# Gates of 32 early steps for the last 128 features of all batches, one stage earlier, in a recurrent kernel on one Trainium2 core

## The chip, the cores and the metric

The kernel runs on one core of a Trainium2 chip. Its engines are named as in the profile: PE (TensorE, matmuls; PEld is its weight load), DVE (VectorE), ACT (ScalarE), POOL (GpSimd) and SP (SyncE, which here issues nearly all DMAs). The metric is the device time of one execution in microseconds (us); lower is better. Everything is float32.

## The reference

Input x has 16 batches, 512 steps and 512 features; a condition vector of 512 features goes with each batch. Four layers, each added to its input:

```python
x = x + (x + x * sigmoid(silu(cond @ W1.T + b1) @ W2.T + b2))     # what the first layer comes to here
x = x + hs          # h_t = tanh(x_t @ Wx + h_{t-1} @ Wh + b), h_0 = cond
x = x + hidden      # gated scan, below
x = x + x + x @ (base + A_b @ B_b.T)     # A_b, B_b: rank 8, made from cond by a small network
```

The third layer is the one that the change touches:

```python
forget_gate = sigmoid(x @ W_f.T + b_f)
input_gate  = sigmoid(x @ W_i.T + b_i)
gate_sum = forget_gate + input_gate + EPS
forget_norm = forget_gate / gate_sum
new_info = input_gate / gate_sum * (x @ W_h.T + b_h)
# hidden: a scan over the 512 steps with forget_norm + EPS and new_info, started from cond
```

`forget_norm` and `new_info` at a step depend only on x of that step, so they can be made as soon as the second layer has that step. The scan itself needs all steps.

## The kernel before

Features lie on partitions in KC = 4 chunks of 128; x2 (the input of the third layer) stays in SBUF as [128, 4, 16 batches, 512 steps].

**The recurrence.** 512 steps in NBLK = 64 blocks of T = 8 steps. One step on PE is 16 recurrent products (`accumulate`, line 371, with `wh_sb`; in the profile L371 pre<-wh_sb,h_out; 32 matmul records), then ACT takes tanh in four pieces (L535), DVE transposes them into h (L536), and only then can the next step's recurrent matmuls start. Engines work through their instructions in program order, which is written out by hand here. Between the recurrent matmuls of two steps PE is given other work, the filler of a step, in this order:
- `inputs` of the next block: 16 units a block, divided among the steps by SHARE (lines 480 to 487);
- `layer_part` (line 318; matmuls L332): in blocks 0 to 16, four times a block, one layer of the network that makes A and B. Its weights come in chunks of 256 KB, loaded AHEAD = 3 chunks ahead by `load_chunk` (L316), each load issued when a chunk has been used;
- `early_gate` (line 402; matmuls L418): one quarter (one of four 128-feature products) of a gate for the early steps.

**Early gates.** SETS lists which (batches, steps, feature chunk j) are made during the recurrence. A set is always 512 columns (batches times steps) and takes 12 calls of `early_gate`: four for the forget gate, four for the input gate, four for the candidate. PARTS says at which steps of a block a call stands: none in the first FIRST = 8 blocks, then steps 0, 2, 4 up to block 16, and steps 0, 2, 4, 6 afterwards. A set's sums, reciprocals and products are cut into 16 pieces, which `do_pieces` puts on DVE one a step, behind the step's transposes. The results go to `early` in DRAM (L435) and are loaded again later. The first two sets take 8 batches of 64 steps; they use one PSUM buffer only ("pg"), since the other ("pf") still serves `layer_part`. The tiles `ef`, `ei` and `es` have one buffer each.

**Ends of blocks.** After step 7 of a block n: `end_layer(n)` (line 342) copies a layer's result into a tile "got" (one buffer, DVE, L347) and stores it (four DMAs, L349); two 128-row chunks of the third layer's weights are loaded (L564), wf in blocks 2 and 3, wi in 4 and 5, wc in 6 and 7, base in 8 and 9; and after block 2 `turn_bias` (line 358) transposes the bias b2a on PE, copies it on DVE into another "got" (L363) and stores it (L365). All these DMAs are issued by SP, in this order.

**The batches.** After the recurrence, for each of 16 batches four `gate_unit`s (line 585), one for each feature chunk j: 12 products on PE over the columns from `te` on (L591; `te` is what `made_before` says was made early), two sigmoids, a chain on DVE (among it the reciprocal L608 and three scans over 512 steps), two additions on POOL. `make_layer` (L645, L648) and `last_layer` (L655, 13.7 us of matmuls a batch) of the batch before lie between the units.

Of the kernel before, what the change touches and what calls it, by code (L numbers as in the profile page):

```python
# [30 lines left out]
F32 = mybir.dt.float32  # L31
# [4 lines left out]
P = 128  # L36
B, S, D = 16, 512, 512
KC = D // P
R = 8

T = 8
# [11 lines left out]


WIDE = 512
FIRST, MAIN = 64 // T, 128 // T + 1
SETS = [(slice(8, 16), slice(0, 64), j) for j in (0, 1)]
SETS += [(slice(b, b + 4), slice(0, 128), j) for b in (0, 4) for j in range(KC)]
SETS += [(slice(b, b + 4), slice(0, 128), j) for b in (8, 12) for j in (2, 3)]
SETS += [(slice(b, b + 4), slice(64, 192), j) for b in (8, 12) for j in (0, 1)]  # L60

PARTS = [()] * FIRST + [(0, 2, 4)] * (MAIN - FIRST) + [(0, 2, 4, 6)] * (NBLK - MAIN - 1) + [(0, 2, 3, 4, 6)]
# [15 lines left out]
def kernel(  # L78
# [54 lines left out]
    w2pool = rnn.enter_context(tc.tile_pool(name="w2pool", bufs=1))  # L133
# [72 lines left out]
    with tc.tile_pool(name="pre", bufs=1, side="right") as pre, tc.tile_pool(  # L206
        name="ps_pre", bufs=1, space=PSUM
# [92 lines left out]
    ps_q = rnn.enter_context(tc.tile_pool(name="ps_q", bufs=1, space=PSUM))  # L300
# [57 lines left out]
    def turn_bias():  # L358

        turned = ps_q.tile([P, P], F32, tag="pg", name="b2a_turned")  # L360
        nc.tensor.transpose(turned, b2a_raw.rearrange("p k r -> p (k r)"), ident)
        got = w2pool.tile([P, P], F32, tag="got", name="b2a_got")
        nc.vector.tensor_copy(got, turned)  # L363
        for c in range(KC):
            nc.sync.dma_start(out=bias_a[:, c * P : (c + 1) * P], in_=got[c * BP : c * BP + R, :])  # L365
# [33 lines left out]
    def early_gate(q, step):  # L399

        u, k = divmod(q, KC)
        number, which = divmod(u, 3)
        batches, steps, j = SETS[number]
        shape = dict(b=batches.stop - batches.start, t=steps.stop - steps.start)
        first = number < 2
        if k == 0:

            pool, tag = ((ps_q, "pg"), (ps_p, "pf"))[0 if first else u % 2]
            early_gate.ps = pool.tile([P, WIDE], F32, tag=tag, name=f"pg_{u}")
            if which == 0:  # L410
                early_gate.tiles = [
                    w2pool.tile([P, WIDE], F32, tag=name, name=f"{name}_{number}")
                    for name in ("ef", "ei", "es")
                ]
        ps = early_gate.ps
        w = (wf_sb, wi_sb, wc_sb)[which]
        for c in range(KC):
            nc.tensor.matmul(  # L418
                ps[c * BP : (c + 1) * BP, :].rearrange("p (b t) -> p b t", **shape),
                w[:, k, j * P + c * BP : j * P + (c + 1) * BP],  # L420
                x2[:, k, batches, steps],
                start=(k == 0),
                stop=(k == KC - 1),
                skip_group_check=True,
            )
        if k < KC - 1:
            return
        f, i, s = early_gate.tiles
        halves = [slice(n * WIDE // 2, (n + 1) * WIDE // 2) for n in range(2)]

        def sigmoid(gate, bias):
            nc.scalar.activation(gate, ps, AF.Sigmoid, bias=col(bias, j))

        def store(which, got):
            nc.sync.dma_start(  # L435
                out=early[batches, which, j, :, steps].rearrange("b p t -> p b t"),
                in_=got.rearrange("p (b t) -> p b t", **shape),
            )

        def total(at):  # L440
            nc.vector.scalar_tensor_tensor(s[:, at], f[:, at], EPS, i[:, at], ALU.add, ALU.add)

        def invert(at):
            nc.vector.reciprocal(s[:, at], s[:, at])

        def normalize(which, at):
            got = (f, i)[which]
            nc.vector.tensor_tensor(got[:, at], got[:, at], s[:, at], ALU.mult)
            if at is halves[1]:
                store(which, got)  # L450

        def times_candidate(at):
            nc.vector.scalar_tensor_tensor(
                i[:, at], ps[:, at], col(C_BH, j), i[:, at], ALU.add, ALU.mult
            )
            if at is halves[1]:
                pieces.extend(lambda at=at: normalize(1, at) for at in halves)

        def end_input_gate():
            sigmoid(i, C_BI)  # L460
            early_gate.sums = [lambda at=at: total(at) for at in halves]
            pieces.extend(early_gate.sums)
            for n in range(8):
                at = slice(n * WIDE // 8, (n + 1) * WIDE // 8)
                pieces.append(lambda at=at: invert(at))
            pieces.extend(lambda at=at: normalize(0, at) for at in halves)

        if which == 0:

            timed.setdefault(step if first else step + 6, []).append(lambda: sigmoid(f, C_BF))  # L470
        elif which == 1:
            timed.setdefault(step, []).append(end_input_gate)
        else:

            assert not any(job in pieces for job in early_gate.sums)
            urgent.extend(lambda at=at: times_candidate(at) for at in halves)
# [23 lines left out]
    for n in range(NBLK):  # L500
        ahead = []
        if n + 2 < NBLK:
            xs.append(new_x1(n + 2))
        for s in range(T):
            odd = s % 2
            g = next(i for i, pair in enumerate(PAIRS) if s in pair)
            for k in range(KC):
                for j in range(KC):
                    accumulate(pre, g, j, h_prev[:, k, :], wh_sb[:, k, :])
            if n == 0 and s < G - 1:  # L510
                for k in range(KC):
                    inputs(0, (s + 1) * KC + k, pre)

            if n + 1 < NBLK:
                if n == 1 and s in LATE:
                    for i in range(*LATE[s]):
                        inputs(n, i, pre)
                for i in range(*SHARE[n][s]):
                    inputs(n + 1, i, nxt)
            if s in LAYER_STEPS[n]:  # L520
                layer_part(n, LAYER_STEPS[n].index(s))
            if s in PARTS[n]:
                early_gate(made, n * T + s)
                made += 1
            a = apool.tile([P, P], F32, tag="a", name=f"a_{n}_{s}")

            h = h_out[s]
            if odd:
                turned, h_prev = h[:, :, :BP], h[:, :, B:]
            else:  # L530
                turned, h_prev = h[:, :, B:], h[:, :, :BP]
            bank, place = PLACE[g]
            for c in range(KC):
                at = slice(c * BP, (c + 1) * BP)
                nc.scalar.activation(a[:, at], pre[bank][:, place, at], AF.Tanh)  # L535
                nc.vector.transpose(turned[:, c, :], a[:, at])  # L536
            if s == max(PAIRS[g]):
                t0, t1 = PAIRS[g]
                step = t1 - t0
                at = slice(n * T + t0, n * T + t1 + step // abs(step), step)  # L540
                nc.vector.tensor_tensor(  # L541
                    x2[:, :, :, at].rearrange("p k b t -> p k t b"),
                    xs[n][:, :, t0 // 2, :, :],
                    turned.rearrange("p k (t b) -> p k t b", t=2),
                    ALU.add,
                )
            elif n + 2 < NBLK:
                gated(nc.vector, xs[n + 2], xb, s)
                if s == G - 1 and n + 3 < NBLK:
                    xb = load_x(n + 3)  # L550
            if s in BEGINS:
                if s < T - 1 and 0 < n < NBLK - 1:
                    nxt.append(begin(n + 1, BEGINS[s]))
                elif s == T - 1 and n + 2 < NBLK:
                    ahead.append(begin(n + 2, BEGINS[s]))
            do_pieces(n * T + s)
        if n < len(LAYERS):
            end_layer(n)

        for i in (2 * n - 4, 2 * n - 3):  # L560
            if 0 <= i < 4 * KC:
                which, k = divmod(i, KC)
                w_sb, w = ((wf_sb, wfT), (wi_sb, wiT), (wc_sb, wcT), (base_sb, base))[which]
                nc.sync.dma_start(out=w_sb[:, k, :], in_=w[k * P : (k + 1) * P, :])  # L564
        if n == 2 * KC + 4:
            for k in range(KC):
                diag = base_sb[:, k, k * P : (k + 1) * P]
                nc.vector.scalar_tensor_tensor(diag, ident, 2.0, diag, ALU.mult, ALU.add)
        if n == 2:
            turn_bias()  # L570
        pre, nxt = nxt, ahead
# [165 lines left out]
```

## Time and profile before

| what | value |
|---|---|
| median of 3 runs | 1641.43 us (1639.55 to 1641.94) |
| the profiled execution | 1640.39 us, its span 1638.6 us |
| recurrence: first recurrent matmul to last | 16.6 to about 914 us |
| a step without an early gate, blocks 4 to 7 | 1.64 us |
| a step with early gates in its block, blocks 17 on | 1.73 and 1.75 us in turn |
| reciprocal L608 over 384 and 320 columns | 2552 and 2153 ns |

A step's time is the distance between the first transposes (L536) of two steps in the timeline. In the profile's group rows, the text before the bar names line, engine, operation, what is written and what is read, and how often; after it stand the busy time in us and the mean of one in ns, then the idle time before these instructions and what ended it. A timeline row gives start and length in us, engine, line, operation, and in brackets the idle time before it with its releaser. A row of the table of stretches gives the stretch, its length, then the busy time and count of PE, PEld, DVE, ACT and POOL, the granted PE clock, the DMA engines' share and GB/s.

### The profile page before, as it was taken

The page shows a single profiled execution, that of the slowest core. Times are in us where ns is not written, and L with a number is a line of the kernel's source. Part 1 is how long each engine was busy: PE and PEld are TensorE (multiplying, and loading weights), DVE is VectorE, ACT ScalarE, POOL GpSimd, SP SyncE. Part 2 cuts the span into 40 slices and gives each one's busy share as a digit, 9 for nine tenths or more (in the row PEclk, how much of TensorE's full clock was granted, in tenths as well). Part 3 has the DMA queues.
Part 4 walks back from the last instruction along what each step waited for, and adds up shares of the span by engine and source line. Part 5 has one row for each costly group of instructions (what it writes and reads, how often), then busy time and mean ns, then how long its engine had stood idle before and what let it go on. Part 6 is the DMA issues. An engine that isn't in the chain of part 4 may idle for free.

```text
span 1638.6 us, 67294 instructions
## 1 busy us (share of the span) xinstructions
PE 1610.1 (98%) x29117; PEld 1135.8 (69%) x29117; DVE 1132.8 (69%) x3592; ACT 419.3 (26%) x2476; POOL 173.0 (11%) x144
## 2 busy tenths in 40 slices
PE   7899999999999999999999999999999999999998
PEld 6788888888888888888888555555555555555553
DVE  3444655565555656566565798888888888899886
ACT  3233333333333333333333111111111111111111
POOL 0000000000000000000000022212121222222221
PEclk9999999999999999999999999999999999999999
DMA  5344432111111111111110001101111111111111
GB/s 188 112 148 144 127 108 53 36 37 36 36 33 34 36 36 36 37 36 36 36 37 23 26 23 39 41 32 41 38 41 38 44 43 43 39 34 37 44 36 57
DMA packets 106042, 86.05 MB, mean 53 GB/s; under 512 B 15072, under 2 KB 84224, under 8 KB 105744
## 3 DMA queue, kind: packets, MB, share of 16 engines
q1 hardware_dynamic: 104640, 81.66, 16.3%
q8 instruction: 228, 3.74, 0.9%
q14 instruction: 70, 0.57, 0.1%
q10 hardware_dynamic: 1104, 0.08, 0.0%
HBM read 54.95 MB, written 26.76 MB: 50 GB/s over the span
## 4 chain that ended last, share of the span: by engine, by line
PE 90%; DVE 6%; issue 2%; ACT 1%; DMA 1%; POOL 0%; SPq 0%; DVEq 0%; ACTq 0%; POOLq 0%
PE pre L371 41%; PE po L655 11%; PE pg L418 11%; PE pf L591 8%; PE pi L591 8%; PE pc L591 8%; DVE s L608 1%; PE pl L645 1%; PE pf L332 1%; DVE s L620 1%; DVE s L616 1%; DVE i L619 0%; DVE h_out L536 0%; ACT a L535 0%; DVE f L622 0%
## 5 line engine op out<-in xcount | busy, mean ns | idle before, releaser
L371 PEld LDWEIGHTS pre<-wh_sb,h_out 128*32 128x32 f32 x16384 | 456.4, 110 | 157.8 <-DVE h_out L536 154.7
L371 PE MATMUL pre<-wh_sb,h_out 128*32 128x128 f32 x16384 | 548.1, 274 | 10.4 <-DVE h_out L536 6.3
L536 DVE STREAM_TRANSPOSE h_out<-a 128x32 f32<-128x32 f32 x2048 | 264.8, 187 | 357.8 <-ACT a L535 356.7
L535 ACT ACTIVATE a<-pre 128x32 f32<-128x32 f32 x2048 | 238.0, 203 | 584.9 <-PE pre L371 584.9
L371 PE MATMUL pre<-wx_sb,x 128*32 128x128 f32 x8192 | 282.0, 274 | 2.4 <-DVE x L169 2.1
L371 PEld LDWEIGHTS pre<-wx_sb,x 128*32 128x32 f32 x8192 | 233.4, 111 | 3.2 <-issue 3.1
L655 PE MATMUL po<-layer,x 128*128 128x512 f32 x480 | 208.7, 592 | 0.8 <-POOL x L627 0.8
L591 PE MATMUL pf<-x,wf_sb 128*128 128x384 f32 (+1 forms) x512 | 170.7, 476 | 1.8 <-DVE x L541 1.3
L655 PEld LDWEIGHTS po<-layer,x 128*128 128x128 f32 x480 | 91.1, 190 | 112.0 <-issue 106.9
L591 PE MATMUL pc<-x,wc_sb 128*128 128x384 f32 (+1 forms) x512 | 168.8, 473 | 0.0
L591 PE MATMUL pi<-x,wi_sb 128*128 128x384 f32 (+1 forms) x512 | 168.8, 473 | 0.0
L608 DVE RECIPROCAL s<-s 128x384 f32<-128x384 f32 (+1 forms) x64 | 157.0, 2453 | 2.1
L591 PEld LDWEIGHTS pf<-x,wf_sb 128*128 128x128 f32 x512 | 95.7, 190 | 75.1 <-issue 17.3
L626 POOL TENSOR_TENSOR s<-s,f 128x512 f32<-128x512 f32 x63 | 86.5, 1373 | 520.4 <-DVE s L620 501.5
L591 PEld LDWEIGHTS pi<-x,wi_sb 128*128 128x128 f32 x512 | 97.3, 190 | 61.0
L591 PEld LDWEIGHTS pc<-x,wc_sb 128*128 128x128 f32 x512 | 97.3, 190 | 61.0
L541 DVE TENSOR_TENSOR x<-x,h_out 128x128 f32<-128x128 f32 x256 | 101.2, 395 | 18.7
L606 ACT ACTIVATE f<-pf,vec_sb 128x384 f32<-128x384 f32 (+1 forms) x64 | 36.4, 568 | 289.9 <-POOL s L626 142.6
L659 ACT COPY osb<-po 128x512 f32<-128x512 f32 x64 | 37.5, 585 | 263.4 <-PE po L655 122.3
L607 DVE SCALAR_TENSOR_TENSOR s<-f,i 128x384 f32<-128x384 f32 (+1 forms) x64 | 35.7, 558 | 92.0 <-ACT i L606 90.9
L579 POOL MEMSET zero<- 128x1 f32 x1 | 0.1, 98 | 915.3 <-DMA early<-ei 915.3
L627 POOL TENSOR_TENSOR x<-s,x 128x512 f32<-128x512 f32 x63 | 83.6, 1328 | 4.9
(84 smaller groups left out, 1186.9 us busy)
## 6 DMA issues: line engine op xcount, KB each, us to landing
w<-in_l3w_dram SPq DMA_DIRECT2D x68, 256.0 KB
xb<-in_xT_dram SPq DMA_DIRECT2D x64, 256.0 KB
out_dram<-osb SPq DMA_DIRECT2D x64, 256.0 KB
early<-ef SPq DMA_DIRECT2D x18, 256.0 KB
early<-ei SPq DMA_DIRECT2D x18, 256.0 KB
f<-early SPq DMA_DIRECT2D x48, 64.0 KB
i<-early SPq DMA_DIRECT2D x48, 64.0 KB
f<-early SPq DMA_DIRECT2D x16, 96.0 KB
```

The lines of the kernel that those rows point to most:

```text
L371: nc.tensor.matmul(pre[PLACE[g][0]][j * BP : (j + 1) * BP, PLACE[g][1], :], lhsT, tile_columns(w, j), start=False, stop=False, skip_group_ ...
L418: nc.tensor.matmul(ps[c * BP : (c + 1) * BP, :].rearrange("p (b t) -> p b t", **shape), w[:, k, j * P + c * BP : j * P + (c + 1) * BP], x2 ...
L535: nc.scalar.activation(a[:, at], pre[bank][:, place, at], AF.Tanh)
L536: nc.vector.transpose(turned[:, c, :], a[:, at])
L541: nc.vector.tensor_tensor(x2[:, :, :, at].rearrange("p k b t -> p k t b"), xs[n][:, :, t0 // 2, :, :], turned.rearrange("p k (t b) -> p k ...
L591: nc.tensor.matmul(p[:, te:], w_sb[:, k, j * P : (j + 1) * P], x2[:, k, b, te:], start=(k == 0), stop=(k == KC - 1),)
L606: nc.scalar.activation(gate[:, new], p[:, new], AF.Sigmoid, bias=col(bias, j))
L608: nc.vector.reciprocal(s[:, new], s[:, new])
L626: engine.tensor_tensor(s, s, f, ALU.add)
L627: engine.tensor_tensor(x3[:, j, :], s, x2[:, j, b, :], ALU.add)
L655: nc.tensor.matmul(po, x3[:, k, at], layer[:, k, :], start=(k == 0), stop=(k == KC - 1))
L659: nc.scalar.copy(osb, po)
```

## The change

There are three edits.

A new first set: the last 128 features (j = 3) of all 16 batches for steps 0 to 31. It takes blocks 4 to 7, since FIRST becomes 4; SHARE follows FIRST, so the inputs in blocks 4 to 7 go to the steps that blocks 8 to 16 use. The sets that came before for j = 3 with steps 0 to 127 now take steps 32 to 159. The number of sets grows from 18 to 19, and each set from the third on moves accordingly (blocks 8 to 15 keep theirs). In the batches `te` of j = 3 becomes 160 where it was 128, for all batches.

The weights' loads after the blocks come one block earlier: wf after blocks 1 and 2, wi after 3 and 4, wc after 5 and 6, base after 7 and 8.

The copy of b2a goes to the first 128 columns of the tile "es" instead of "got".

```diff
-FIRST, MAIN = 64 // T, 128 // T + 1
-SETS = [(slice(8, 16), slice(0, 64), j) for j in (0, 1)]
-SETS += [(slice(b, b + 4), slice(0, 128), j) for b in (0, 4) for j in range(KC)]
-SETS += [(slice(b, b + 4), slice(0, 128), j) for b in (8, 12) for j in (2, 3)]
+FIRST, MAIN = 32 // T, 128 // T + 1
+SETS = [(slice(0, 16), slice(0, 32), KC - 1)]
+SETS += [(slice(8, 16), slice(0, 64), j) for j in (0, 1)]
+NSETS = len(SETS)
+SETS += [(slice(b, b + 4), slice(0, 128), j) for b in (0, 4, 8, 12) for j in range(KC - 1) if b < 8 or j > 1]
+SETS += [(slice(b, b + 4), slice(32, 160), KC - 1) for b in (0, 4, 8, 12)]
 SETS += [(slice(b, b + 4), slice(64, 192), j) for b in (8, 12) for j in (0, 1)]
...
-        got = w2pool.tile([P, P], F32, tag="got", name="b2a_got")
+
+        got = w2pool.tile([P, WIDE], F32, tag="es", name="b2a_got")[:, :P]
...
-        first = number < 2
+        first = number < NSETS
...
-            pool, tag = ((ps_q, "pg"), (ps_p, "pf"))[0 if first else u % 2]
+            pool, tag = ((ps_q, "pg"), (ps_p, "pf"))[0 if first else (u - 3 * NSETS) % 2]
...
-        for i in (2 * n - 4, 2 * n - 3):
+        for i in (2 * n - 2, 2 * n - 1):
```

## The prediction, made before the changed kernel was run

> **What bounds the kernel now.** I read the page first: busy shares, the chain that ended last, the costliest groups.
>
> ```profile
> PE 1610.1 (98%) x29117; PEld 1135.8 (69%) x29117; DVE 1132.8 (69%) x3592; ACT 419.3 (26%) x2476; POOL 173.0 (11%) x144
> ...
> PE 90%; DVE 6%; issue 2%; ACT 1%; DMA 1%; POOL 0%; SPq 0%; DVEq 0%; ACTq 0%; POOLq 0%
> ...
> L371 PEld LDWEIGHTS pre<-wh_sb,h_out 128*32 128x32 f32 x16384 | 456.4, 110 | 157.8 <-DVE h_out L536 154.7
> ```
>
> TensorE is busy 98% and holds 90% of the chain, but in two different ways. In the recurrence (to 914 us) it waits 155 us for the transposes of h: a step is recurrent matmuls, tanh, transposes, and the filler (input projections, gates made early) lies beside tanh and transposes. Of an early gate only what exceeds that gap costs time. In the batches after 914 us nothing hides matmuls. The table of stretches of time, for batch 2 (four units of 384 columns) and for batch 11 (two of 384, two of 320):
>
> ```profile
> 1010.82:1056.78 45.96, 45.96 (x137) 24.55 (x137) 39.90 (x49) 6.67 (x12) 10.78 (x8) 1.00 0.11 38
> 1414.23:1457.64 43.41, 43.41 (x138) 24.56 (x137) 37.37 (x45) 6.47 (x12) 10.65 (x8) 1.00 0.13 42
> ```
>
> The first number is the length, the second TensorE's busy time, the fourth VectorE's (39.90 and 37.37, so 86%). TensorE has no gap: a column left out there is time won.
>
> The list of waits has one odd row, b2a_got on factor, 4.5 us. VectorE's timeline shows its price:
>
> ```profile
> 59.29 0.49 DVE L536 STREAM_TRANSPOSE h_out<-a 128x32 f32<-128x32 f32 x4 [0.73 <-ACT a L535]
> ...
> 60.22 0.29 DVE L347 TENSOR_TENSOR got<-pf,b 128x128 f32<-128x128 f32 x1
> 64.97 0.29 DVE L363 COPY b2a_got<-b2a_turned 128x128 f32<-128x128 f32 x1 [4.46 <-DMA factor<-got]
> 65.18 0.48 DVE L536 STREAM_TRANSPOSE h_out<-a 128x32 f32<-128x32 f32 x4
> ...
> 67.67 0.49 DVE L536 STREAM_TRANSPOSE h_out<-a 128x32 f32<-128x32 f32 x4 [1.83 <-ACT a L535]
> ...
> 69.67 0.46 DVE L536 STREAM_TRANSPOSE h_out<-a 128x32 f32<-128x32 f32 x3 [1.34 <-ACT a L535]
> ```
>
> The copy shares the single buffer "got" with layer 2's factors and waits until their stores have landed; the next step's transposes are queued behind it. From 59.29 to 69.67 are three steps, 10.38 us; three ordinary ones of this stage take 4.93.
>
> [...] the 32 matmuls after a gap of 4.08 us took 1.94 us, otherwise 1.08. So the wait costs more than its 4.46. [...] Here the 8 records of one early gate, 592 ns each, span 1.07 us. [...] These loads go through SP's queue; two weight loads issued from 121.18 were moved by about 124.2 (below)[...]. [...] The trace's packets show 27 ns for 512 B, 18 for 256 and 13 for 128.
>
> **The change, part by part.**
> 1. b2a in "es". The copy then has only the transpose to wait for; "es" has no earlier user, and its next, the first set's sums, comes in block 6. VectorE is free at 60.51, tanh for the next step begins at 60.99, the copy takes 0.29 and ends before it. Gain 10.38 - 4.93 = 5.45 us. What could be late next is SP: factor stores (4), weights (2), b2a (4), biases (4) stand before block 3's first chunk load, some 7 us from 60.5, so it is issued at about 67.5 and lands by about 70. Its matmuls come at about 72.9. I take 5.4; bounds 4 and 5.5.
>
> 2. Blocks 4 to 7 get 12 early gates (48 matmuls of 512 columns), two sigmoids on ScalarE and 16 VectorE pieces; inputs go to other steps as in blocks 8 to 16. The trace has the twin of such blocks. The first transposes of blocks 4, 8, 12 and 16 stand at:
>
> ```profile
> 79.54 0.49 DVE L536 STREAM_TRANSPOSE h_out<-a 128x32 f32<-128x32 f32 x4 [0.43 <-ACT a L535]
> ...
> 132.51 0.49 DVE L536 STREAM_TRANSPOSE h_out<-a 128x32 f32<-128x32 f32 x4 [0.54 <-ACT a L535]
> ...
> 190.38 0.49 DVE L536 STREAM_TRANSPOSE h_out<-a 128x32 f32<-128x32 f32 x4 [0.38 <-ACT a L535]
> ...
> 246.88 0.49 DVE L536 STREAM_TRANSPOSE h_out<-a 128x32 f32<-128x32 f32 x4 [0.38 <-ACT a L535]
> ```
>
> Four blocks without early gates took 52.97 us, four with the first set 57.87 (with the one load of the sigmoid table, 1.28, which the new first set takes over), four with the second set 56.50. After the change blocks 4 to 15 are one stretch of the middle kind and two of the last: 57.87 + 56.50 + 56.50 - 167.34 = 3.5 us added. 48 matmuls at 1.07 us for four would be 12.8: three quarters hides in the transposes' gap. Bounds 2.8 (four blocks of 13.9 against 52.97 without the pauses that both have) and 5 (a pause of TensorE without a wait, of up to 0.88 in block 8, in each block).
>
> 3. Weights one block earlier. For the gate of block 4 (wf, loaded after blocks 1 and 2) and block 5 (wi) this is ample. The last two chunks of wc are loaded after block 6, and chunk 2 is needed at step 2 of block 7. In block 8 of the trace the gate of step 2 begins at 135.50, 3.50 after the factor stores began (132.00). After block 6 in the trace:
>
> ```profile
> 118.85 2.29 SPq L349 DMA_DIRECT2D factor<-got  x4
> 121.18 0.90 SPq L564 DMA_DIRECT2D wc_sb<-in_wcT_dram  x2
> ```
>
> The gate would come at 118.85 + 3.50 = 122.35; the load is issued at 121.18 [...]. By the bytes of each microsecond (109 GB/s in 122 to 123, 394 in 123 to 124) the first 256 KB are moved at 123.4[...]. TensorE, in order, waits about 1.45 us; 0.6 of it is the gap in which it waits for transposes anyway (the gates' idle time there, 0.60). Cost 0.9; bounds 0 and 2. Behind the waiting gate stands the next step's recurrent matmul, and behind that everything. Chunk 3 is due two steps later and is in time. The first pair of wc (after block 5, due at step 4 of block 6) also is.
>
> 4. Stores of the first set: 128 B runs, 2,048 pieces twice. 2048 x 13 ns / 16 engines = 1.7 us each, against 1.15 for 1,024 of 256 B (the second set). They stand in block 8 ahead of one chunk load, which has some 2.4 us to spare (in block 4 that load is issued at 86.06, lands at about 88.6 and is used at 91.01). Cost 0; bounds 0 and 1.
>
> 5. Afterwards 32 columns fewer in unit j = 3 of each batch. 128 columns fewer took 45.96 - 43.41 = 2.55 us, so 32 take 0.64. VectorE, by the groups by shape: (2552 - 2153) ns of the reciprocal and about 0.07 to 0.11 for each of four others over 64 columns, half of it 0.36 us. In the first batch TensorE waits for the last unit of VectorE and GpSimd at 964.9, so 0.36. In the chain of waits, the last two batches (from 1543.7) run through VectorE: 0.36 each. 13 x 0.64 + 3 x 0.36 = 9.4. Bounds 5.8 (VectorE throughout) and 10.2 (TensorE throughout). The early reads grow from 512 to 640 B a row in the same number of pieces; they lie beside matmuls.
>
> Sum: -5.4 + 3.5 + 0.9 + 0 - 9.4 = -10.4 us. The profiled execution took 1640.39 (span 1638.6), giving 1630.0. The median of the three runs is 1641.43, that is 1.0 higher; I forecast between, 1630.5.
>
> **Rivals.**
> - VectorE sets the pace of the batches. For it: 86% busy, and it holds the chain's end. Against: no gap in TensorE in the middle batches, and VectorE is shortened too. Item 5 becomes 5.8: 1634.1.
> - A new wait takes part of the old one's place: wc's chunk 2 at 2 us, or block 3's chunk load at 2 to 3 us, since nothing pauses any more while SP catches up. For it: SP is some 5 us behind at a block's start (in block 4 TensorE has done the first layer part by 81.54, and the chunk load that it frees is issued at 86.06). Against: both margins above. About 2.5 us back: 1633.
> - Slower: chunk loads late in each block from 4 on. If SP's issues fall 2.4 us further behind, each of the 16 layer parts of blocks 4 to 7 waits; at 0.9 us each that adds 14.4: 1644.9. Below those 2.4 us it costs nothing. Against: per block nothing is added to SP but two stores, and the blocks get longer.
>
> **How the numbers follow.** Forecast 0.66, VectorE 0.12, new wait 0.17, slower 0.05. Low end: no wait for wc (0.9), item 2 at 2.8, item 5 at 10.2, together 2.4 below, and a little for the pauses: 1627.5. High end takes in the first two rivals: 1634.5. Within 0.2% (3.3 us, about what can be told from no change) needs two mishaps. Faster 0.94, same 0.02, slower 0.04.
>
> **What would show it.** No b2a row in the waits and steps of 1.64 us there; blocks 4 to 7 at 13.9 us with one longer step near block 7's step 2 and a wait of TensorE on wc; batches of 45.3 and 42.8 us. Wrong if the middle batches shrink by 0.36 us, if weight-chunk matmuls (L332) wait, or if the sigmoid of the second set waits for the first set's store.

## The result, and the profile after

The changed kernel takes 1637.05 us (median of 16 runs, 1634.06 to 1640.89), beside 1641.53 for the kernel before in the same session (16 runs, 1638.75 to 1645.18). The ratio is 0.9972, 95% interval 0.9964 to 0.9980. It is faster, by 4.5 us where 10.4 had been worked out; the range on record ended at 1634.5. The profiled execution took 1637.08 us (span 1635.3), so it stands for the median. The one before took 1640.39, 1.1 below its median, so the two profiles differ by 3.3 us where the medians differ by 4.5.

The page shows little of what is missing. Busy shares, the chain by engine and the largest group:

```profile
PE 1609.0 (98%) x29213; PEld 1142.2 (70%) x29213; DVE 1132.4 (69%) x3608; ACT 419.5 (26%) x2478; POOL 172.5 (11%) x144
...
PE 91%; DVE 5%; issue 2%; DMA 1%; ACT 1%; POOL 0%; SPq 0%; DVEq 0%; POOLq 0%; ACTq 0%
...
L374 PEld LDWEIGHTS pre<-wh_sb,h_out 128*32 128x32 f32 x16384 | 461.6, 110 | 152.6 <-DVE h_out L539 148.1
```

The idle time before these loads fell by 5 us (157.8 to 152.6), about what b2a promised, and the shares stand still. So the span has to be taken apart by stages, from the first transposes of one block to those of another, in both traces:

| stretch | before | after | difference | predicted |
|---|---|---|---|---|
| start, blocks 0 and 1 | 47.58 | 48.29 | +0.7 | 0 |
| blocks 2 and 3 (b2a) | 31.96 | 27.92 | -4.0 | -5.4 |
| blocks 4 to 15 (new set) | 167.3 | 175.0 | +7.7 | +4.4 |
| blocks 16 and 17 | 28.22 | 27.84 | -0.4 | 0 |
| blocks 18 to the end of the last step | 638.2 | 638.2 | 0 | 0 |
| batches | 725.3 | 718.0 | -7.3 | -9.4 |
| span | 1638.6 | 1635.3 | -3.3 | -10.4 |

**b2a.** VectorE's timeline after block 2 (start, length, engine, line, operation):

```profile
60.86 0.29 DVE L349 TENSOR_TENSOR got<-pf,b 128x128 f32<-128x128 f32 x1
61.07 0.28 DVE L366 COPY b2a_got<-b2a_turned 128x128 f32<-128x128 f32 x1
...
62.39 0.49 DVE L539 STREAM_TRANSPOSE h_out<-a 128x32 f32<-128x32 f32 x4 [1.04 <-ACT a L538]
```

The copy follows the factors with no bracket, that is with no wait, and the transposes come 1.0 us after the copy's end; they are no longer queued behind it for 4.5 us. That part works as written. In the trace before, TensorE's granted clock was 0.50 from 64.8 to 68.2 us, at the end of the gap of 4.08 us and behind it; here there is no such gap, and the clock is 1.00 from 60 to 70.

**Blocks 4 to 15.** The list of waits of this kernel from 15 to 300 us (engine and tile, released by what: us, times, longest) has three rows that are new or grown:

```profile
PEld pre L374 <- issue: 8.0, 13, 2.5
DVE x L171 <- DMA xb<-in_xT_dram: 4.1, 2, 2.4
...
PEld pg L421 <- DMA wc_sb<-in_wcT_dram: 2.0, 1, 2.0
```

The third is the wait for wc that was predicted, at double its price. The second stood at 2.0 us, once, before, at the kernel's start; the wait that is new is for x of block 9. The first, 5.2 us in 5 before, is TensorE standing still while nothing that the profile knows is missing. The largest of these lies in block 4, in the timeline of weight loads:

```profile
87.21 0.15 PEld L374 LDWEIGHTS pre<-wh_sb,h_out 128*32 128x32 f32 x4
89.23 0.69 PEld L374 LDWEIGHTS pre<-wh_sb,h_out 128*32 128x32 f32 x26 [1.87 <-issue]
```

In the middle of 30 loads for one step, with h there, 1.87 us pass. Such pauses also sit in the last steps of blocks 2 and 3 (2.36 and 2.31 us; 1.93 and 1.64 where b2a alone is changed, below). Blocks 2 and 3 together gained 1.4 us less than b2a's 5.4.

**The wait for wc**, in the chain of work through 120 to 128 us:

```profile
122.46 0.42 SPq L351
...
122.92 3.37 DMA wc_sb<-in_wcT_dram
...
126.33 1.06 PE pg L421 x8
```

The load leaves SP right behind the factor stores and takes 3.37 us from issue to landing. The wc load behind block 6 in the trace before, issued at 121.18, landed at 123.86 (the last of its 16 landing events), in 2.68 us. For the gate at 122.35 that is a wait of 1.51 us, close to the 1.45 that the author had estimated; in the changed kernel the load took longer. And the step lasted 3.63 us instead of 1.73, longer by nearly all of the 1.95 us that the gate's weight loads waited. The prediction had taken off 0.6 us for a gap in which TensorE waits for transposes anyway. The next step with a gate shows what that gap is:

```profile
129.84 1.04 PE L421 MATMUL pg<-x,wc_sb 128*32 128x512 f32 x8
130.58 0.90 PEld L374 LDWEIGHTS pre<-wh_sb,h_out 128*32 128x32 f32 x32 [0.61 <-DVE h_out L539]
```

The 0.61 us is idle time of the weight loads, and the gate's own matmuls run through it, to 130.88. A wait ahead of the gate moves these matmuls too, so nothing can be hidden there.

**x for block 9.** SP's queue in the changed kernel, while the new set's results are stored (`early<-ef`, `early<-ei`, pieces of 128 bytes):

```profile
140.49 0.38 SPq L438 DMA_DIRECT2D early<-ef  x1
140.91 4.81 SPq L328 DMA_DIRECT2D b<-in_b2b_dram  x4
145.82 0.37 SPq L318 DMA_DIRECT2D w<-in_l3w_dram  x1
146.30 0.39 SPq L438 DMA_DIRECT2D early<-ei  x1
146.78 2.32 SPq L318 DMA_DIRECT2D w<-in_l3w_dram  x1
149.19 0.39 SPq L152 DMA_DIRECT2D xb<-in_xT_dram  x1
```

A store costs SP 0.38 us itself here; it is the next issue that is held. Four bias loads take 4.81 us together, 1.83 in block 8 of the kernel before, and one weight load 2.32 where 0.4 is usual. The load of x behind them leaves at 149.19, and VectorE waits for it, with the transposes behind it:

```profile
154.33 0.29 DVE L171 TENSOR_TENSOR x<-xb,g 128x128 f32<-128x128 f32 x1 [2.38 <-DMA xb<-in_xT_dram]
154.54 0.48 DVE L539 STREAM_TRANSPOSE h_out<-a 128x32 f32<-128x32 f32 x4
```

That step took 3.08 us instead of 1.73.

**The batches.** The table of stretches for batches 2 and 11, as in the prediction (length, then busy time of PE, PEld, DVE, ACT, POOL; clock, DMA share, GB/s):

```profile
998.18:1043.50 45.32, 45.32 (x137) 24.55 (x136) 38.95 (x46) 6.62 (x12) 10.76 (x8) 1.00 0.12 38
1398.39:1441.16 42.77, 42.77 (x138) 24.55 (x137) 36.74 (x45) 6.41 (x12) 10.62 (x8) 1.00 0.13 43
```

Each is 0.64 us shorter and TensorE has no gap: the step of the prediction seems right twice. But from batch 8 on VectorE does not keep up. Its reciprocals (L611) come 43.05 us apart a batch from batch 8 on, against TensorE's 42.76; from the start of a batch's third unit to its reciprocal it is 6.6 us in batch 7 and 8.6 in batch 14, where before it was 6.6 in all of these. Buffers absorb the lag until batch 14, which takes TensorE 47.01 us where it was 45.10 before: the 1.9 us of lag fall due at once. VectorE is 86% busy, as before, so it isn't full. The timeline in batch 13 shows what it waits for:

```profile
1511.35 1.20 DVE L623 TENSOR_TENSOR_SCAN s<-i,zero 128x512 f32<-128x512 f32 x1
1512.58 0.32 SPq L608 DMA_DIRECT2D i<-early  x1
1512.63 1.26 POOL L629 TENSOR_TENSOR s<-s,f 128x512 f32<-128x512 f32 x1 [5.79 <-DVE s L623]
...
1513.92 0.32 SPq L608 DMA_DIRECT2D f<-early  x1
...
1514.29 3.24 SPq L663 DMA_DIRECT2D out_dram<-osb  x3
...
1516.59 0.59 ACT L662 COPY osb<-po 128x512 f32<-128x512 f32 x1 [7.87 <-DMA out_dram<-osb]
1517.07 0.59 ACT L609 ACTIVATE f<-pf,vec_sb 128x384 f32<-128x384 f32 x1
1517.55 0.58 ACT L609 ACTIVATE i<-pi,vec_sb 128x384 f32<-128x384 f32 x1
1518.24 0.56 DVE L610 SCALAR_TENSOR_TENSOR s<-f,i 128x384 f32<-128x384 f32 x1 [5.69 <-ACT i L609]
```

Read it as a ring. VectorE's scan and GpSimd's addition free the tiles i and f (their ends, 1512.55 and 1513.89, are the moments at which SP issues the early loads into them). The output's store stands behind these loads on SP. Its landing, 2.30 us after its issue, frees one of two output tiles; ScalarE's copy waits for that, and the sigmoids of the next unit, long computed on TensorE, stand behind the copy. VectorE waits for the sigmoids, and its scan frees i again.

The trace also has TensorE's granted clock at 0.50 from 1573.9 to 1577.3, just after batch 14. It costs nothing that shows: the last batch takes 61.60 us here and 61.59 in the mended version below, whose trace has no such stretch there.

So 7.1 us are missing: 2.1 in the batches, 1.0 on wc, 1.3 on x, and 2.7 put down to pauses as what is left (1.4 in blocks 2 and 3, 1.0 in blocks 4 to 15, 0.3 elsewhere).

### The profile page after: what moved, and what is told of

Read it like the earlier page. It is cut to its first block, busy times and chain, and to the rows that moved or that the text cites. A ratio compares the mean times of both kernels' runs of the same rounds, so it can differ in the third digit from the quotient of the medians.

```text
span 1635.3 us, 67511 instructions
## 1 busy us (share of the span) xinstructions
PE 1609.0 (98%) x29213; PEld 1142.2 (70%) x29213; DVE 1132.4 (69%) x3608; ACT 419.5 (26%) x2478; POOL 172.5 (11%) x144
## 3 DMA queue, kind: packets, MB, share of 16 engines
q8 instruction: 229, 3.75, 1.0%
## 4 chain that ended last, share of the span: by engine, by line
PE 91%; DVE 5%; issue 2%; DMA 1%; ACT 1%; POOL 0%; SPq 0%; DVEq 0%; POOLq 0%; ACTq 0%
PE pre L374 41%; PE po L658 12%; PE pg L421 12%; PE pf L594 8%; PE pi L594 8%; PE pc L594 8%; DVE s L611 1%; PE pl L648 1%; PE pf L334 1%; DVE s L623 1%; DVE s L619 1%; DVE i L622 0%; DMA w_sb<-in_w1T_dram 0%; DMA xb<-in_xT_dram 0%; DVE f L625 0%
## 5 line engine op out<-in xcount | busy, mean ns | idle before, releaser
L374 PEld LDWEIGHTS pre<-wh_sb,h_out 128*32 128x32 f32 x16384 | 461.6, 110 | 152.6 <-DVE h_out L539 148.1
L594 PE MATMUL pf<-x,wf_sb 128*128 128x384 f32 (+2 forms) x512 | 168.9, 473 | 2.3 <-DVE x L544 1.3
L594 PE MATMUL pc<-x,wc_sb 128*128 128x384 f32 (+2 forms) x512 | 165.3, 466 | 0.0
L594 PE MATMUL pi<-x,wi_sb 128*128 128x384 f32 (+2 forms) x512 | 165.3, 466 | 0.0
L611 DVE RECIPROCAL s<-s 128x384 f32<-128x384 f32 (+1 forms) x64 | 153.7, 2402 | 2.1
L662 ACT COPY osb<-po 128x512 f32<-128x512 f32 x64 | 37.5, 586 | 265.7 <-DMA out_dram<-osb 115.6
```

Source lines behind the costliest of these rows:

```text
L374: nc.tensor.matmul(pre[PLACE[g][0]][j * BP : (j + 1) * BP, PLACE[g][1], :], lhsT, tile_columns(w, j), start=False, stop=False, skip_group_ ...
L594: nc.tensor.matmul(p[:, te:], w_sb[:, k, j * P : (j + 1) * P], x2[:, k, b, te:], start=(k == 0), stop=(k == KC - 1),)
L611: nc.vector.reciprocal(s[:, new], s[:, new])
L662: nc.scalar.copy(osb, po)
```

## The experiments

Two readings were open. For the batches: the ring through the output tiles, or VectorE's own work as the bound. For the pauses: DMA traffic that holds something back which TensorE needs, or the order of the new instructions. The rest sizes the parts. Each ratio is to the kernel before on the same chip, with its 95% interval; "step (7, 2)" is step 2 of block 7.

**b2a alone.** On the kernel before:

```diff
-        got = w2pool.tile([P, P], F32, tag="got", name="b2a_got")
+        got = w2pool.tile([P, WIDE], F32, tag="es", name="b2a_got")[:, :P]
```

> The kernel before with only the copy of b2a moved to the tile es. Theory 1 (the wait cost what the three long steps show): steps around 60 us fall from 10.4 to about 5 us, the time falls by 5.4 us to about 1636. Theory 2 (without that pause TensorE meets other pauses right after, as blocks 2 to 4 of the changed kernel show): it falls by 3 us or less, and steps of 2 us and more without a named releaser stand in blocks 2 to 4.

1637.59 us, ratio 0.9978 (0.9971 to 0.9986), that is -3.7. In its profile blocks 2 and 3 take 26.58 us, 5.4 below the kernel before. That this is to the tenth what had been worked out is partly luck: the three long steps went from 10.38 to 5.21, 5.2 us, and the other 0.2 is a pause that one more step had before. The last step ends 6.5 us earlier, since fewer pauses happened to fall before it. In the last batch some of the output's matmuls then come 0.85 us apart instead of 0.43, with the granted clock at 0.51 from 1617.4 to 1620.8, and 1.8 us are given back. The median agrees with this one edit giving nearly all that the whole change gives: the new set as it stands is worth next to nothing.

**wc one block earlier still.** On the changed kernel:

```diff
-        for i in (2 * n - 2, 2 * n - 1):
+        for i in {4: (6, 7, 8), 5: (9, 10, 11), 6: ()}.get(n, (2 * n - 2, 2 * n - 1)):
```

> The changed kernel with wc loaded one to two blocks earlier (its four chunks after blocks 4 and 5, nothing after 6). If the wait on wc in block 7 cost its 1.9 us, the step of 3.63 us there becomes 1.73 and the time falls by 1.9 us to about 1635. If more loads at once after block 5 hold TensorE up elsewhere, a longer step appears in block 6 and the time falls by less than 1 us.

1634.07 us, ratio 0.9958 (0.9945 to 0.9970). The row of wc is gone from the waits and step (7, 2) is ordinary; blocks 4 to 7 take 58.77 us, 61.08 in the changed kernel. The batches are untouched (reciprocals 43.05 us apart). Block 6, behind the added loads, took 15.08 us for 14.10, with two pauses of 0.56 and 0.53 us. In the mended version below, with the same edit, it took 13.99, so they are not shown to come with the loads. The two kernels' intervals overlap, so the size rests on the profile.

**A third output tile.** On the changed kernel:

```diff
-            osb = work.tile([P, D], F32, tag="osb", name=f"osb_{b}_{t}")
+            osb = work.tile([P, D], F32, tag="osb", name=f"osb_{b}_{t}", bufs=3)
```

> The changed kernel with three output buffers osb in place of two. Theory 1 (from batch 8 on a ring sets the pace: the copy of an output waits for an output store to land, the store stands in SP's queue behind loads of early gates that wait for GpSimd, and the sigmoids stand behind the copy): with a buffer more the reciprocals of batches 8 to 14 keep the distance of TensorE's 42.76 us instead of 43.05, the last batches lose less, and the time falls by 1.5 to 2.5 us. Theory 2 (VectorE's own chain of dependent instructions needs 43.05 us a batch): no change, 1637.

1633.79 us, ratio 0.9954 (0.9941 to 0.9966). The timeline of the same place:

```profile
1510.34 0.59 ACT L662 COPY osb<-po 128x512 f32<-128x512 f32 x1 [2.85 <-PE po L658]
1512.92 0.58 ACT L609 ACTIVATE f<-pf,vec_sb 128x384 f32<-128x384 f32 x1 [2.00 <-PE pf L594]
1515.45 0.58 ACT L609 ACTIVATE i<-pi,vec_sb 128x384 f32<-128x384 f32 x1 [1.95 <-PE pi L594]
```

Copy and sigmoids now wait for TensorE alone. Reciprocals come 42.76 us apart, the lag stays at 6.6, batch 14 takes 45.10 again, and the batches are 2.7 us shorter. The ring is shown as the cause: only a buffer was added to it, and VectorE's work is the same.

**The same tile on the kernel before.** The same edit there:

> The kernel before with a third output buffer. Theory 1 (the ring through the output copies is hidden there behind TensorE's longer batches and decides only in the changed kernel's batches from 8 on): only the first two batches gain, 0 to 1 us, about 1640.6. Theory 2 (the ring holds the kernel before as well): it gains as much as the changed kernel did with this buffer, 2.7 us or more.

1639.71 us, ratio 0.9993 (0.9985 to 1.0001). Only the first full batch is shorter (47.68 for 48.56); the others keep 45.96 and 43.40. Before, the ring was hidden. By how little can be estimated: the change took 0.36 us of VectorE's work out of each turn, so it turned in about 43.05 + 0.36 = 43.41 us, just TensorE's 43.40.

**No chunk loads.** On the changed kernel, loads of the network's weights after the first three are left out, and its layers use the old chunks again:

```diff
+        if m >= AHEAD:
+            chunk_sb.append(chunk_sb[m - AHEAD])
+            return
```

> The changed kernel without the loads of the fourth layer's weight chunks after the first three; the later layers use these three again, so the output's fourth layer is computed with wrong weights and 16 MB of DMA traffic are left out in blocks 0 to 16. Theory 1 (TensorE's pauses without a releaser in blocks 1 to 15, about 7 us in sum in the changed kernel, come from its instructions being fetched late behind other transfers): the pauses fall below 1.5 us in sum and the time by 5 to 6 us, to about 1631. Theory 2 (they have nothing to do with the transfers): they stay, and the time moves by less than 1 us.

1633.39 us, ratio 0.9951 (0.9938 to 0.9965). In the row "PEld pre <- issue" the pauses up to 300 us, the first of 2.5 us at the start left out, fall from 5.5 to 3.0 us, and the two large ones left (1.09 and 0.77 us) stand while the 128-byte stores run. So DMA traffic seems to take part in them. The gain from 1637.05, 3.7 us, lies between the two theories' numbers, and not all of it is pauses: with fewer loads in SP's queue, x for block 9 came in time and step (9, 0) took 1.73 us instead of 3.08.

**Spare traffic where it is quiet.** On b2a alone, one 256 KB load more a step in blocks 24 to 39, which nobody reads:

```diff
+            if 24 <= n < 40:
+                spare = w2pool.tile([P, D], F32, tag="w2", name=f"spare_{n}_{s}", bufs=AHEAD)
+                which, r = LAYERS[1 + (n - 24)]
+                nc.sync.dma_start(out=spare, in_=l3w2[which, r][s % KC * P : (s % KC + 1) * P, :])
```

> The kernel before with b2a in es and, in blocks 24 to 39, a spare load of 256 KB a step that nobody reads (128 loads, 32 MB). Nothing is added on TensorE, VectorE or ScalarE. Theory 1 (TensorE's pauses without a releaser are late instruction packets behind other transfers): pauses of 0.3 to 2 us appear in these blocks, 2 us or more in sum, each ending 1.2 to 1.5 us after an instruction packet's end, and the time is 1639.5 or more. Theory 2 (they belong to the start of the kernel or to its other waits): these blocks stay at 13.91 us, 1637.6.

1641.22 us, ratio 1.0007 (0.9998 to 1.0016), beside 0.9978 for b2a alone: some 4 us. The stretch from 365 to 590 us of this kernel, and the waits in it:

```profile
365.00:590.00 225.00, 223.49 (x6631) 183.37 (x6625) 134.13 (x727) 76.86 (x566) 0.00 (x0) 1.00 0.56 174
```

```profile
PEld pre L371 <- issue: 2.6, 5, 1.1
```

The same stretch of b2a alone, in whose waits there is no such row:

```profile
365.00:590.00 225.00, 225.00 (x6723) 184.81 (x6716) 136.09 (x736) 77.95 (x575) 0.00 (x0) 1.00 0.13 36
```

174 GB/s instead of 36, nothing waits for the data, and TensorE has pauses. Blocks 24 to 39 take 226.04 us instead of 222.88. Traffic alone brings pauses where there were none.

**The earlier loads without the set.** On b2a alone, the third layer's weights one block earlier:

```diff
-        for i in (2 * n - 4, 2 * n - 3):
+        for i in (2 * n - 2, 2 * n - 1):
```

> The kernel before with b2a in es and with the weights loaded one block earlier, no new set. Theory 1 (the pauses of blocks 1 to 4 in the changed kernel come with the earlier loads): the first four blocks take 1 to 2 us longer than with b2a alone, and the time is 1638 to 1639. Theory 2 (they come with the early gates themselves): blocks 0 to 3 and 4 to 7 as with b2a alone (55.3 and 52.7 us), 1637.6.

1637.12 us, ratio 0.9975 (0.9965 to 0.9985), the same as b2a alone. Blocks 0 to 7 agree within 0.5 us. The earlier loads cost nothing by themselves; only the new set's due times make wc late.

**Longer pieces for the new set's stores.** On the changed kernel the new set goes to a tensor of its own, in one piece of 2 KB a partition, and each unit j = 3 loads it with a DMA of its own:

```diff
+            if number == 0:
+                nc.sync.dma_start(out=early0[which].rearrange("p b t -> p (b t)"), in_=got)
+                return
...
-            nc.sync.dma_start(out=gate[:, old], in_=early[b, which, j, :, old])
+            if j == KC - 1:
+                nc.sync.dma_start(out=gate[:, :32], in_=early0[which, :, b, :])
+                nc.sync.dma_start(out=gate[:, 32:te], in_=early[b, which, j, :, 32:te])
+            else:
+                nc.sync.dma_start(out=gate[:, old], in_=early[b, which, j, :, old])
```

> The changed kernel with the new first set's results stored in a tensor of their own, 2 KB in one piece for each partition (128 pieces a store in place of 2,048), and loaded from there later in two loads for a row. Theory 1 (the 128-byte pieces hold up SP's next issue by 2 to 3 us each and with it the load of x in block 8): no instruction on SP of more than 1.5 us after the stores, step 0 of block 9 is 1.73 us without the wait on xb, gain 1.3 to 2 us, about 1635.5. Theory 2 (SP waits there for something else): its long issue stays, no gain. More loads in the batches could cost some of it through SP's queue.

1640.74 us, ratio 0.9994 (0.9986 to 1.0002), slower than the changed kernel. Its SP queue in block 8:

```profile
139.56 0.37 SPq L440 DMA_DIRECT2D early<-ef  x1
139.97 1.86 SPq L329 DMA_DIRECT2D b<-in_b2b_dram  x4
```

The bias loads take 1.86 us instead of 4.81 and step (9, 0) is ordinary, so the small pieces did hold SP. The first issue behind the first of the two stores took 2.1 to 3.7 us in the five traces with 128-byte pieces, and 0.43 in the two with long ones. But two more loads for each unit j = 3 stand in the ring ahead of the output's store: reciprocals 43.5 us apart instead of 43.05. This run doubles as a test of the ring from the other side: more on SP makes it slower.

**Mended versions.** The changed kernel with the third tile and the earlier wc, first with the longer pieces, then without:

> The changed kernel with three output buffers, wc after blocks 4 and 5, and the first set stored in rows. If the causes are separate their gains add up (2.7 for the buffer, 1.9 for wc, 1.3 for the rows): 5.9 us below the changed kernel, about 1631. If TensorE's pauses take up what is freed: 1633 or more.

> The changed kernel with three output buffers and wc after blocks 4 and 5, without the storing in rows. Theory 1 (the long issue on SP behind the 128-byte stores costs 1.3 us in block 9, also when the rest is mended): 1 to 1.5 us slower than the version with rows, about 1632.2, and step 0 of block 9 is near 3 us. Theory 2 (the rows gain nothing): 1631.

With them 1630.95 us, ratio 0.9937 (0.9925 to 0.9948); without, 1631.01 us, 0.9940 (0.9928 to 0.9953). In the second, step (9, 0) still takes 3.03 us, yet the times agree: the longer pieces earn nothing that can be measured. Its blocks 4 to 7 take 56.7 us, 61.1 in the changed kernel (1.9 of the 4.4 is the wait for wc, the rest pauses that this execution did not have), and from the first unit to the end it takes 714.1, 717.0 there. The third tile and the earlier wc make up the version to keep, faster than both kernels.

**The third tile with b2a, without the set:**

> The kernel before with b2a in es and three output buffers, without the new set and the earlier loads. If the new set is worth what the batches save (about 10 us) less what blocks 4 to 7 cost (4 us, and some 2 us of pauses), this version takes 1636.5 and lies 4 to 5 us above the mended version with the set. If the set is worth nothing: 1632 or less.

1635.35 us, ratio 0.9971 (0.9961 to 0.9982). Against 0.9940 with the set and the earlier wc, in the same session: the set, once it is mended, is worth 0.3%, 4.3 us by the medians.

## Why the prediction was wrong

Two steps failed: the stores of 128-byte pieces at no cost (item 4), and a column left out as time won through all middle batches (item 5). The wait for wc was mis-sized (item 3), and nothing was put into the sum for more pauses of TensorE (3.2 us before, 6.7 after, from 17 to 290 us).

1. **b2a, -5.4.** Mechanism and size are right in the steps (5.2 us in the three steps, 5.38 in blocks 2 and 3 of b2a alone). In the changed kernel 1.4 of it was lost there, most of it to pauses. That the median of b2a alone fell by 3.7 only fits the 1.8 us that its one profile loses in the last batch; whether other executions lose it there isn't shown.
2. **Blocks 4 to 7, +3.5.** The twin holds: 13.93 us for an undisturbed block with the new set, in the mended version's block 4. More pauses than before were in the bounds (+5), not in the value.
3. **wc, +0.9.** The mechanism, the chunk and the step are right; the term was mis-sized, 1.9 (2.1 to 3.1 in the three other profiles with the late load). Of its parts, the landing took 3.37 us where the trace before had 2.68, and the 0.6 us were no gap of TensorE: they were idle time of the weight loads beside the gate's own matmuls.
4. **The 128-byte stores, 0.** This step failed. They were priced by the DMA engines' time and looked harmless for the one chunk load behind them. The price is on the issuing queue, which was held for 1.7 to 3.2 us behind the first of these stores. The victim is the load of x, which the prediction did not name: 1.3 us here, 0.6 to 1.3 in the three other profiles where it came late.
5. **The batches, -9.4.** Here is the largest miss, 2.1 us. "TensorE has no gap: a column left out there is time won" holds in full for batches 2 to 7. In batches 8 to 13 each saves its 0.64 too, but the ring falls behind by 0.29 a batch, and batch 14 pays 1.9 back. Batches 8 to 14 together won 1.9 us where the sum had 4.2. The rival "VectorE sets the pace" had the right 0.36 us a batch there (43.41 to 43.05), but not the cause: VectorE is not full, it is one member of a ring that a third tile opens. The list of waits before held the row of output copies waiting for their stores (99.7 us in 15; 115.6 in 20 in the changed kernel, none with the third tile), and it was passed over. With the third tile in both kernels the batches take 724.4 us without the set and 715.2 with it: the 9.2 us that had been forecast as 9.4.

The rival of a new wait was right about wc, in part. Late weight chunks did not come. The misses are of one sign: for steps 4 and 5 the sum took values at or near the favourable end of their bounds, and for added pauses none at all.

## What to carry to other kernels

A stage that is full on one engine may have a next limit just beneath it: before counting a saving at the full engine's price, follow one turn of the buffers (who frees the tile, which queue its store stands in, who is queued behind the copy) and compare its length with the stage's. Price a DMA by what its queue's next instruction waits, not by the bytes alone: here four bias loads took SP 4.81 us behind 128-byte pieces and 1.86 behind long ones, for the same bytes. And transfers whose data nobody waits for can still cost TensorE time: here 174 GB/s in place of 36 made 16 blocks 3.2 us longer (226.04 for 222.88).

## What the runs showed of the hardware

TensorE's instructions seem to be brought by DMA themselves. The trace's DMA records hold packets of 16 KB on a queue that the page marks "instruction" (q8: 229 packets, 3.75 MB in the changed kernel). In the quiet blocks of the changed kernel, from 300 to 900 us, they come 4.28 us apart on average, one for 257 records of matmuls and weight loads; from 930 to 1600 us, where these records are fewer, one comes every 40.9 us, for 262 of them. So they follow TensorE's instructions, and under traffic they seem to cost it time. Pauses of over 0.4 us from 36 to 560 us in which nothing is waited for, with the last such packet before TensorE goes on (us; the pause is the idle time of the weight loads):

```
kernel             pause            last packet      end to resume   since the packet before
changed            73.98 - 74.66    72.24 - 73.18    1.48            4.74
changed            87.36 - 89.23    87.00 - 87.96    1.27            5.40
changed            153.19 - 154.03  151.68 - 152.60  1.43            5.23
spare traffic      420.67 - 421.48  419.30 - 420.26  1.22            5.82
spare traffic      425.65 - 426.77  424.39 - 425.34  1.44            5.09
```

In the 13 traces of this case there are 43 such pauses of the weight loads; 42 end 1.21 to 1.55 us after the end of a packet, one 1.63 after, and 39 of these packets came later than the average. But the distance to the packet before does not decide: in the changed kernel 16 packets between 300 and 900 us came 5.0 us or more after the one before, and no such pause followed. That TensorE waited for its instructions is inferred from these times and from the run with spare traffic; no run moved the packets alone. The pauses fall differently in every execution: from 17 to 290 us those of over 0.15 us make 1.4 to 4.8 us in the six profiles without the new set, and 3.0 to 8.3 in the six that have it and all chunk loads.

The second surprise is the issuing queue: behind a store of 2,048 pieces of 128 bytes, SP's following issues took 4.81 us for four and 2.32 for one, against 1.86 and 0.38 behind stores in long pieces. The hold varies: over the five traces the issue right behind the second store took 0.9 to 2.3 us.
